# Attention scores of one head in one PSUM bank, issued in rounds of three matmuls, in a two-layer Mamba, attention and expert kernel

## The chip, the cores and the metric

The kernel runs on one core of one Trainium2 chip. The metric is the device time of one execution in microseconds. A core has five engines that run their own queues in order: TensorE (PE, matrix products into the accumulation memory PSUM), VectorE (DVE), ScalarE (ACT, table functions), GpSimd (POOL) and SyncE (SP, which issues DMAs). PSUM has eight banks; a bank holds 512 fp32 values for each of 128 partitions.

## The reference

A sequence of 2048 tokens of width 128 goes through four blocks, each with a layernorm ahead and a residual sum behind:

```python
x = x + mamba2(layernorm(x))        # 8 heads of 32, state 16: chunked state-space block with gate
nx = layernorm(x)                   # 16 heads of 8, causal attention
scores = einsum('bqhd,bkhd->bhqk', q, k) / sqrt(8)
x = x + softmax(where(causal, scores, min)) @ v @ Wo + bo
nx2 = layernorm(x)                  # 8 experts, the best two of each token, gates by softmax
for e in range(8):
    h = gelu(nx2 @ fc1_w[e].T + fc1_b[e])
    moe += (h @ fc2_w[e].T + fc2_b[e]) * dense_gates[..., e:e+1]
x = x + moe
x = x + mamba1(layernorm(x))        # h = dA * h + dB*u, state 16, summed over the state
x = x + mlp(layernorm(x))           # silu(w1 x) * (w2 x), two gelu layers, w3
```

## The kernel before

The 2048 tokens lie in four chunks of 512 (`C`). Each block handles a chunk at a time; causal attention of chunk `c` reads the keys of chunks 0 to `c`. Everything is traced in one program, so the order in which Python generators are advanced is the order of every engine's queue. The functions `ssd` (first block), `attentions`, `experts`, `scan` (third block) and `feed` (last block) are such generators; each `yield` carries a weight of planned work. `with_attention` advances the stages of other blocks and, for each weight it gets times `RATE`, steps of attention. So attention's instructions lie between those of the state-space block of later chunks, and later between those of experts, scans and feed-forward of earlier chunks. When attention ends, the tail runs: `scan(2)` with `experts(3)`, `scan(3)` with `feed(2)`, and `feed(3)` alone. Within attention, `in_step` advances two generators in turn:

- `weighted(c, g)` works on a group `g` of four heads. For each block of 128 keys it makes the transposed scores (line 352), adds each query's shift by a matmul with ones (line 358), adds the causal mask on the diagonal by a matmul (line 360), takes the exponential on ACT (line 362), and, one key block later, multiplies with the values (`sum_up`, line 339).
- `shift(c, g)` is one group ahead. It makes the scores a second time, with queries on the partitions (line 302), adds the mask (line 311), and takes the maximum over the keys on DVE (line 312); the negated maxima, split in two parts, are the shift that `weighted` adds.

A head has 8 features. With a split of each operand into high and low parts it fills 32 partitions, so the score matmuls of four heads lie on four row groups of PE, and those that are issued together run at once. Both generators work on pairs of heads: a tile of two banks takes the scores of heads `i` and `i + 1`, and one ACT or DVE instruction reads both (128 x 1024 values).

PSUM is shared out by tags (line 81): `m` has one buffer of two banks (the maximum's scores and attention's small products), `e` one of two banks (the weighted scores), `o` one bank (the sum over values), `a` two banks and `c` one bank (the other blocks). `whole` (line 141) gives a one-bank request the two-bank buffer of `m` or `e`. A `Stream` (line 657) names the tags that a stage of the second layer uses: `bank` goes round its `tags`, `sum` takes its `sums`. Stages beside attention use `a` and, for sums, `c`; in the tail `other` uses `m`, `e` and, for sums, `o`.

In `experts`, the gates of the chunk are transposed to rows (lines 757 to 774, with a high and a low part). For each expert a matmul `spread_row` copies one row to all 128 partitions (line 719), DVE copies it out (line 785), four products with GELU follow (lines 789, 790), then the second product (line 794) and its weighting by the gate (line 796). Weights come by SP's DMAs (lines 780, 781), and SP also fetches the broadcast rows `bb` of the scan (line 861) from a scratch in DRAM.

Of the kernel before, what the change touches and what calls it, by code (L numbers as in the profile page):

```python
# [12 lines left out]
F32 = mybir.dt.float32  # L13
# [59 lines left out]
def two_layers(ctx: ExitStack, tc: tile.TileContext, a: dict, out: bass.AP):  # L73
# [7 lines left out]
    BUFS = {"m": 1, "e": 1, "o": 1, "a": 2, "c": 1}  # L81
# [58 lines left out]

    def whole(tag, shape):
        if tag in ("m", "e") and len(shape) == 2 and shape[1] == C:
            return psum(tag, [shape[0], 2, C])[:, 0]
        return psum(tag, shape)
# [103 lines left out]

    def prepare(c):
# [13 lines left out]
        for g in range(0, NG, 2):  # L263
            qR.append(ak.tile([P, 2, C], F32R, tag="qR", name="qR", bufs=3))
            for w, n, dst in ((w_k, "k", kR[:, g : g + 2, cs]), (w_q, "q", qR[-1])):
                pf = psum("m" if n == "k" else "e", [P, 2, C])
                for j in range(2):
                    nc.tensor.matmul(pf[:, j], w[:, g + j], nT, start=True, stop=True)
                    hi = ak.tile([P, C], F32R, tag="os", name="hi")
                    nc.scalar.activation(hi, pf[:, j], AF.Identity, bias=col(f"b{n}", g + j))  # L270
                    nc.tensor.matmul(pf[:, j], minus[n], hi, start=False, stop=True, skip_group_check=True)
                    nc.vector.tensor_scalar(dst[:, j], pf[:, j], col(f"b{n}", g + j), None, ALU.add)
                yield 2.2
# [13 lines left out]
    def shift(c, g):  # L287
# [4 lines left out]
        for r in range(NB):  # L292
            w = (r + 1) * P
            top = sp.tile([P, 4, c + 1], F32, tag="top", name="top", bufs=4)
            for kc in range(c + 1):
                diag = kc == c
                n = w if diag else C
                for i in (2, 0):
                    pss = psum("m", [P, 2, C])
                    for j in range(2):  # L300
                        hr = slice(32 * (i + j), 32 * (i + j) + 32)
                        nc.tensor.matmul(  # L302
                            pss[:, j, 0:n],
                            qR[hr, w - P : w],
                            kR[hr, g, kc * C : kc * C + n],
                            start=True,
                            stop=not diag,
                        )
                    yield None
                    for j in range(2 * diag):  # L310
                        nc.tensor.matmul(pss[:, j, w - P : w], ident16, mask_qk, start=False, stop=True)
                    nc.vector.tensor_reduce(top[:, i : i + 2, kc], pss[:, :, 0:n], AX.X, ALU.max)  # L312
                    yield 0.4
# [13 lines left out]
    def weighted(c, g):  # L327
# [15 lines left out]

        for kb in range(nk):
# [3 lines left out]
            for i in range(0, 4, 2):  # L348
                pss = psum("e", [P, 2, C])
                for j in range(2):  # L350
                    hr = slice(32 * (i + j), 32 * (i + j) + 32)
                    nc.tensor.matmul(  # L352
                        pss[:, j, q0:], kR[hr, g, kb * P : (kb + 1) * P], qR[hr, q0:], start=True, stop=False
                    )
                yield None
                for j in range(2):
                    hr = slice(32 * (i + j), 32 * (i + j) + 32)
                    nc.tensor.matmul(pss[:, j, q0:], onesR[hr], sh[hr, q0:], start=False, stop=not diag)  # L358
                for j in range(2 * diag):
                    nc.tensor.matmul(pss[:, j, q0 : q0 + P], ident16, mask_kq, start=False, stop=True)  # L360
                pr = ak.tile([P, 2, C], F32, tag="probs", name="probs", bufs=3)
                last = nc.scalar.activation(  # L362
                    pr[:, :, q0:], pss[:, :, q0:], AF.Exp, scale=float(1.0 / np.sqrt(np.float32(HD)))
                )
                in_turn("exp", last)
                prs.append(pr)
                yield None

                if i == 0 and waiting:
                    sum_up(*waiting.pop())  # L370
                yield 1.1
            waiting.append((kb, q0, prs, last))
        sum_up(*waiting.pop())
# [81 lines left out]
    with ExitStack() as first:  # L455
# [36 lines left out]
        bigs, smalls = ["a", "a", "e"], ["c", "o", "m"]  # L492

        def big(shape):
            bigs.append(bigs.pop(0))
            return whole(bigs[-1], shape)

        def small_bank(shape):
            smalls.append(smalls.pop(0))
            return whole(smalls[-1], shape)  # L500
# [151 lines left out]
        bigs[:], smalls[:] = ["a"], ["c"]  # L652
# [4 lines left out]
    class Stream:  # L657
# [16 lines left out]
        def bank(self, shape):  # L674
            self.n += 1
            return whole(self.tags[self.n % len(self.tags)], shape)

        def sum(self, shape):
            return whole(self.sums, shape)
# [7 lines left out]
    side = Stream("", wk, 4, 6, ("a",), "c")  # L687
    scans = Stream("s", wk, 8, 4, ("a",), "c")
# [3 lines left out]
    w_bd = load(wp, "w_bd", [P, 2, 3 * DS], "(k p) o -> p k o", p=P)  # L692
    w_u = load(wp, "w_u", [P, 2, DI], "(k p) o -> p k o", p=P)
    w_dt1 = load(wp, "w_dt1", [3 * DS, DI])
# [7 lines left out]

    zeros = side.line("zeros")
    nc.gpsimd.memset(zeros, 0.0)
    two_rows, minus_low, rows_in = {}, {}, {}
    scratch_b = [tc.dram_tile([DS, C], F32, name=f"scratch_b{i}") for i in range(2)]
    for n in (NE,):
        two_rows[n] = wp.tile([P, n], F32R, name=f"two_rows{n}")
        nc.vector.tensor_tensor(two_rows[n], ident[:, 0:n], ident[:, n : 2 * n], ALU.add)
        minus_low[n] = wp.tile([2 * n, 2 * n], F32R, name=f"minus_low{n}")  # L710
# [368 lines left out]
```

## Time and profile before

| | |
|---|---|
| median of three runs | 1753.43 us (1750.17 to 1770.97) |
| profiled execution: its own time, span | 1741.55 us, 1739.8 us |
| mean granted clock of TensorE | 0.837 |
| busy: PE, DVE, ACT, POOL | 1466.9, 975.0, 726.2, 284.0 us |
| first and last exponential (line 362) | 162.7 and 1412.8 us |
| table loads ahead of line 362 | 41, of 1.28 us each |
| maximum (line 312), two full banks | 1222 ns, 224 of 320 |
| exponential (line 362), two full banks | 1024 ns, 224 of 320 |
| score matmuls, 512 columns (lines 302, 352) | 572 and 570 ns in the mean |
| shift matmuls, 512 columns (line 358) | 477 ns in the mean |
| copy of a gate row (line 785) | 24 of 679 ns, 8 in the tail |

The durations of matmuls are modelled from start to the end of their pipeline, and matmuls on different row groups overlap, so the busy time of PE is more than the time for which it takes in columns. The idle time of an engine stands with the instruction before which it stood idle, and behind an arrow what ended it.

### The profile page before, as it was taken

What the parts mean: (1) busy time and instruction counts of PE and PEld (TensorE: products, weight loads), DVE (VectorE), ACT (ScalarE), POOL (GpSimd) and SP (SyncE); (2) the same over time, 40 slices, a digit from 0 to 9 for tenths busy, and PEclk for the clock granted to TensorE, in tenths of its full rate; (3) what the DMA queues carried; (4) which work ended last, traced back from release to release, by engine and by line L of the source; (5) the groups of instructions that cost most, each with busy time, mean ns of one, the idle gap of its engine ahead of it and who ended that gap; (6) DMA issues with size and microseconds to landing.
All of it is one profiled execution on the core that took longest, in us unless ns stands there. A gap on an engine that the chain in (4) does not pass through costs nothing. (4 is left out here: it accounts for less than half of the span.)

```text
span 1739.8 us, 16427 instructions
## 1 busy us (share of the span) xinstructions
PE 1466.9 (84%) x6306; PEld 633.5 (36%) x6306; DVE 975.0 (56%) x1556; ACT 726.2 (42%) x847; POOL 284.0 (16%) x316
## 2 busy tenths in 40 slices
PE   6898999998999888888978887789999888658528
PEld 3554545444333333232333322433333233223214
DVE  4566646557344565667466686674442036774950
ACT  2222322322445444555354454355563536534522
POOL 3322210211000100112111021110000001440220
PEclk9898997887899978889677898669996899868859
DMA  2000000001000000324220045320011022860841
GB/s 85 1 1 1 1 1 1 1 1 55 24 25 25 25 13 21 83 49 103 55 49 14 30 99 107 68 42 25 24 37 31 24 67 78 178 125 31 188 96 30
DMA packets 62494, 83.24 MB, mean 48 GB/s; under 512 B 4576, under 2 KB 28816, under 8 KB 62416
## 3 DMA queue, kind: packets, MB, share of 16 engines
q0 software_dynamic: 16320, 31.46, 10.4%
q1 hardware_dynamic: 45664, 49.68, 9.7%
q8 instruction: 49, 0.80, 0.2%
q10 hardware_dynamic: 432, 1.06, 0.2%
q14 instruction: 29, 0.24, 0.0%
HBM read 49.55 MB, written 1.18 MB: 29 GB/s over the span
## 5 line engine op out<-in xcount | busy, mean ns | idle before, releaser
L362 ACT ACTIVATE probs<-ps_e 128x1024 f32<-128x1024 f32 (+3 forms) x320 | 286.6, 896 | 505.8 <-PE ps_e L358 304.0
L312 DVE TENSOR_REDUCE top<-ps_m 128x2 f32<-128x1024 f32 (+3 forms) x320 | 339.7, 1062 | 280.8 <-PE ps_m L302 164.1
L302 PE MATMUL ps_m<-kR,qR 32*128 32x512 f32 (+3 forms) x640 | 190.1, 523 | 68.0 <-DVE top L312 55.2
L352 PE MATMUL ps_e<-qR,kR 32*128 32x512 f32 (+3 forms) x640 | 175.5, 519 | 27.5 <-ACT probs L362 26.8
L339 PE MATMUL ps_o<-probs,vv 128*9 128x512 f32 (+3 forms) x1152 | 169.7, 599 | 1.0 <-ACT probs L362 0.9
L302 PEld LDWEIGHTS ps_m<-kR,qR 32*128 32x128 f32 x640 | 78.6, 208 | 242.9 <-DVE top L312 132.1
L867 DVE TENSOR_TENSOR_SCAN db<-da,hlast,db 128x512 f32<-128x512 f32 x128 | 163.0, 1310 | 6.5 <-ACT da L863 4.7
L358 PE MATMUL ps_e<-sh,onesR 32*128 32x512 f32 (+3 forms) x640 | 148.9, 431 | 0.0
L352 PEld LDWEIGHTS ps_e<-qR,kR 32*128 32x128 f32 x640 | 69.7, 204 | 182.0 <-ACT probs L362 106.3
L789 PE MATMUL ps_a<-nT,wide 128*128 128x512 f32 x192 | 113.8, 699 | 6.0 <-ACT h L790 3.7
L794 PE MATMUL ps_c<-h,wide 128*128 128x512 f32 x192 | 103.5, 643 | 0.0
L798 POOL TENSOR_TENSOR acc<-acc,ye 128x512 f32<-128x512 f32 x28 | 43.6, 1558 | 331.5 <-DVE ye L796 331.5
L871 POOL COPY hlast<-db 128x2 f32<-128x2 f32 x48 | 29.4, 612 | 378.9 <-DVE db L867 378.9
L863 ACT ACTIVATE da<-dl 128x1024 f32<-128x1024 f32 x64 | 66.4, 1054 | 51.5 <-DMA db<-db 28.3
L865 DVE TENSOR_TENSOR db<-du,bb 128x1024 f32<-128x1024 f32 x64 | 77.9, 1227 | 16.3 <-issue 11.0
L790 ACT ACTIVATE h<-ps_a,cols 128x512 f32<-128x512 f32 x96 | 63.8, 686 | 52.2 <-PE ps_a L789 51.9
L358 PEld LDWEIGHTS ps_e<-sh,onesR 32*128 32x128 f32 x640 | 77.2, 219 | 3.2 <-issue 1.8
L927 PE MATMUL ps_a<-g,wide 128*128 128x512 f32 x96 | 54.0, 690 | 19.5 <-ACT g L930 19.5
L789 PEld LDWEIGHTS ps_a<-nT,wide 128*128 128x128 f32 x192 | 37.1, 215 | 46.3 <-issue 19.5
L362 ACT ACT_TABLE_LOAD x41 | 52.6, 1283 | 1.3 <-PE ps_e L358 0.6
L927 PE MATMUL ps_a<-h,wide 128*128 128x512 f32 x96 | 51.1, 665 | 0.8 <-ACT g L930 0.8
L375 DVE COPY os<-ps_o 128x512 f32<-128x512 f32 x16 | 10.9, 684 | 70.8 <-PE ps_o L339 70.7
(375 smaller groups left out, 2129.3 us busy)
## 6 DMA issues: line engine op xcount, KB each, us to landing
wide<-in_fc SPq DMA_DIRECT2D x64, 256.0 KB, 3.2
bb<-scratch_b SPq DMA_DIRECT2D x64, 256.0 KB, 3.5
db<-db POOLq DMA_DIRECT2D x32, 512.0 KB, 5.7
u<-db POOLq DMA_DIRECT2D x28, 512.0 KB, 6.0
wide<-in_h SPq DMA_DIRECT2D x16, 512.0 KB, 3.7
wide<-in_w SPq DMA_DIRECT2D x8, 256.0 KB, 3.1
x<-in_x SPq DMA_DIRECT2D x4, 256.0 KB, 5.1
w<-in_w SPq DMA_DIRECT2D x4, 256.0 KB, 4.0
```

Of the source, the lines that this page charges most:

```text
L302: nc.tensor.matmul(pss[:, j, 0:n], qR[hr, w - P : w], kR[hr, g, kc * C : kc * C + n], start=True, stop=not diag,)
L312: nc.vector.tensor_reduce(top[:, i : i + 2, kc], pss[:, :, 0:n], AX.X, ALU.max)
L339: pv = nc.tensor.matmul(o, v, prs[i // 2][:, i % 2, q0:], start=kb == 0, stop=kb == nk - 1)
L352: nc.tensor.matmul(pss[:, j, q0:], kR[hr, g, kb * P : (kb + 1) * P], qR[hr, q0:], start=True, stop=False)
L358: nc.tensor.matmul(pss[:, j, q0:], onesR[hr], sh[hr, q0:], start=False, stop=not diag)
L362: last = nc.scalar.activation(pr[:, :, q0:], pss[:, :, q0:], AF.Exp, scale=float(1.0 / np.sqrt(np.float32(HD))))
L789: nc.tensor.matmul(ph, we[:, 0, f * P : (f + 1) * P], nT, start=True, stop=True)
L794: nc.tensor.matmul(py, we[:, 1, f * P : (f + 1) * P], hs[f // 2][:, f % 2, :], start=f == 0, stop=f == NF - 1)
L863: in_turn("exp", nc.scalar.activation(da, dl, AF.Exp, scale=-float(n + 1)))
L865: nc.vector.tensor_tensor(db, du, bb.unsqueeze(1).to_broadcast(two), ALU.mult)
L867: nc.vector.tensor_tensor_scan(db[:, j, :], da[:, j, :], db[:, j, :], hlast[:, j, n : n + 1], ALU.mult, ALU.add)
L927: nc.tensor.matmul(ph, w[k // 2][:, k % 2, f * P : (f + 1) * P], h[k // 2][:, k % 2, :], start=k == 0, stop=k == NF - 1)
```

## The change

Scores now stand in one bank for each head. `m` gets two buffers and `e` three, of one bank each; `c` is gone, and what used it takes `a`.

- In `shift`, each head has its own matmul, its own mask matmul and its own maximum (order 2, 3, 0, 1).
- In `weighted`, a step issues the shift of the head before (`shifted`), then the scores of this head; after the other generator's scores were issued, `finish` issues the mask and the exponential of the head before. `sum_up` follows in the second step of the next key block.
- `in_round` makes each of these matmuls depend on the second last reader noted for `m` and for `e`, so on the maximum and the exponential of two rounds ago.
- `prepare` makes its projections in one bank at a time.
- The rows of the gates go to a scratch in DRAM, and each expert's row comes back by a broadcasting DMA on SP, in place of the spreading matmul and the copy.
- The tail's `other` goes round five buffers of `m` and `e`; the first block's streams go round `a`, `e`, `o` and `m`; 16 unused rows of `bd` are dropped.

```diff
-    BUFS = {"m": 1, "e": 1, "o": 1, "a": 2, "c": 1}
+    BUFS = {"m": 2, "e": 3, "o": 1, "a": 2}
...
+    read = {"m": [], "e": []}
+
+    def in_round(matmul, depth={"m": 2, "e": 2}):
+        for tag, readers in read.items():
+            if len(readers) >= depth[tag]:
+                tc.add_manual_dep(matmul.ins, readers[-depth[tag]].ins.name, SYNC, reason="in one round")
...
-                for i in (2, 0):
-                    pss = psum("m", [P, 2, C])
-                    for j in range(2):
-                        hr = slice(32 * (i + j), 32 * (i + j) + 32)
+                for i in (2, 3, 0, 1):
+                    hr = slice(32 * i, 32 * i + 32)
+                    pss = psum("m", [P, C])
+                    in_round(
                         nc.tensor.matmul(
-                            pss[:, j, 0:n],
...
+                            pss[:, 0:n], qR[hr, w - P : w], kR[hr, g, kc * C : kc * C + n], start=True, stop=not diag
                         )
+                    )
                     yield None
-                    for j in range(2 * diag):
-                        nc.tensor.matmul(pss[:, j, w - P : w], ident16, mask_qk, start=False, stop=True)
-                    nc.vector.tensor_reduce(top[:, i : i + 2, kc], pss[:, :, 0:n], AX.X, ALU.max)
-                    yield 0.4
+                    if diag:
+                        nc.tensor.matmul(pss[:, w - P : w], ident16, mask_qk, start=False, stop=True)
+                    read["m"].append(nc.vector.tensor_reduce(top[:, i, kc : kc + 1], pss[:, 0:n], AX.X, ALU.max))
+                    yield 0.2
...
+        def finish(kb, diag, q0, i, pss, pr):
+            if diag:
+                nc.tensor.matmul(pss[:, q0 : q0 + P], ident16, mask_kq, start=False, stop=True)
+            last = nc.scalar.activation(
+                pr[:, i % 2, q0:], pss[:, q0:], AF.Exp, scale=float(1.0 / np.sqrt(np.float32(HD)))
+            )
+            read["e"].append(in_turn("exp", last))
+            return last
+
+        def shifted(kb, diag, q0, i, pss, pr):
+            hr = slice(32 * i, 32 * i + 32)
+            in_round(nc.tensor.matmul(pss[:, q0:], onesR[hr], sh[hr, q0:], start=False, stop=not diag))
...
+            for i in range(4):
+                hr = slice(32 * i, 32 * i + 32)
+                if i % 2 == 0:
+                    prs.append(ak.tile([P, 2, C], F32, tag="probs", name="probs", bufs=3))
+
+                if begun:
+                    shifted(*begun)
+                pss = psum("e", [P, C])
+                in_round(
+                    nc.tensor.matmul(pss[:, q0:], kR[hr, g, kb * P : (kb + 1) * P], qR[hr, q0:], start=True, stop=False)
+                )
                 yield None
...
+                if begun:
+                    last = finish(*begun)
+                begun = (kb, diag, q0, i, pss, prs[-1])
+
+                if i == 0 and kb:
+                    waiting.append((kb - 1, q_before, prs_before, last))
+                if i == 1 and waiting:
                     sum_up(*waiting.pop())
-                yield 1.1
...
+                yield 0.55
...
-        gT = rows_in[NE][0]
...
+        gT = z.line("gT", (NE, C))
+        nc.vector.tensor_copy(gT, pgt)
+        gates = scratch_g[c % 2]
+        nc.sync.dma_start(gates, gT)
         yield 1.5
...
             we = z.wide()
             nc.sync.dma_start(we[:, 0], a["fc1"][e])
             nc.sync.dma_start(we[:, 1].rearrange("p (k d) -> p k d", k=NF), a["fc2"][e].rearrange("(k p) d -> p k d", p=P))
-            pg = z.bank([P, C])
-            spread_row(pg, NE, gT, e)
             gb = z.line("gb")
-            nc.vector.tensor_copy(gb, pg)
+            nc.sync.dma_start(gb, gates[e].partition_broadcast(P))
...
-        other = Stream("o", pool, 6, 8, ("m", "e"), "o")
+        other = Stream("o", pool, 6, 8, ("m", "e", "m", "e", "e"), "o")
```

## The prediction

> **What bounds the kernel now.** I read the page first, then the windows by stage, then the waits of TensorE (PE), then single rounds in the timeline, and last the costs of single forms.
>
> ```profile
> span 1739.8 us, 16427 instructions
> ...
> PE 1466.9 (84%) x6306; PEld 633.5 (36%) x6306; DVE 975.0 (56%) x1556; ACT 726.2 (42%) x847; POOL 284.0 (16%) x316
> ```
>
> ```profile
> 160.00:1415.00 1255.00, 1123.35 (x5224) 460.72 (x5222) 690.33 (x1073) 556.61 (x642) 154.65 (x172) 0.83 0.15 36
> 1415.00:1740.00 325.00, 211.47 (x540) 95.71 (x538) 193.27 (x243) 135.67 (x147) 79.96 (x68) 0.81 0.47 106
> ```
>
> The columns of the windows are the stretch, its length, then busy time and count of PE, PEld, DVE, ACT and POOL, the granted clock, the DMA share and GB/s. In the attention stage (160 to 1415) PE is busy for 90% of the time and no other engine for over 55%. In the tail (1415 on) it is 65%, and the chain of waits is made of scans, their exponentials and accumulating DMAs. So PE counts before 1415, and a chain through DVE, ACT and DMA after it.
>
> A busy PE is not an efficient one. The timeline shows why, for two neighbouring rounds:
>
> ```profile
> 904.71 0.49 PE L302 MATMUL ps_m<-kR,qR 32*128 32x512 f32 x2
> ...
> 906.77 0.50 PE L302 MATMUL ps_m<-kR,qR 32*128 32x512 f32 x2 [1.09 <-DVE top L312]
> ...
> 907.11 0.39 PE L352 MATMUL ps_e<-qR,kR 32*128 32x512 f32 x2
> ...
> 907.34 0.40 PE L358 MATMUL ps_e<-sh,onesR 32*128 32x512 f32 x2
> ...
> 907.77 1.22 DVE L312 TENSOR_REDUCE top<-ps_m 128x2 f32<-128x1024 f32 x1
> 907.84 1.02 ACT L362 ACTIVATE probs<-ps_e 128x1024 f32<-128x1024 f32 x1 [1.03 <-PE ps_e L358]
> ```
>
> Two things are to be seen. One round takes 906.77 - 904.71 = 2.06 us, because the single m buffer makes PE wait until the 1.22 us maximum has read it. And the six matmuls of 32 rows, which sit on four row groups, came as three batches 0.34 and 0.23 us apart, because m and e came free at different moments. I took the matmuls of lines 302, 352 and 358 of the attention stage in order of start, and called those that start within 30 ns of each other a batch: 903 batches. The ideal is two for each of the 320 rounds, 640; all four score matmuls started together in only 61 rounds.
>
> PE's time in that stage then splits so. Back-to-back fp32 matmuls of 512 columns (L927) start 0.43 us apart at full clock; I take that as their stream, half of it (0.215) for a 32-row batch, and divide by the granted clock. Streams come to 855 us (445 attention, 410 the other work), waits of over 0.35 us to 171, of which 117 stand before attention's score matmuls, and short gaps to 228.
>
> ```profile
> PE ps_m L302 <- DVE top L312: 55.2, 55, 3.6
> ...
> PE ps_e L352 <- ACT probs L362: 26.8, 25, 3.4
> ...
> PE ps_e L789 <- DVE gb L785: 10.5, 3, 4.8
> ...
> PE ps_m L789 <- DVE gb L785: 8.9, 2, 6.3
> ```
>
> These waits (total, times, longest) are PE's own idle time, so they leave out latency inside a matmul. The last two lie in the tail.
>
> **The change, part by part.** The sum is made against the profiled execution's own 1741.55 us; the median of three runs, 1753.43, lies 11.9 above it and I add 12 at the end.
>
> *Batches.* After the change a round is one head: the shift of head i-1, the scores of head i, the maximum's scores of head i+2. These are three row groups and three banks, issued with nothing between them, and the first waits for both the maximum and the exponential of two rounds ago, so the others find their events done. That is about 640 batches, plus some 64 where maxima run alone as a block gets longer: 704 in place of 903. One batch less saves 0.215/0.84 = 0.26 of stream and 0.105 of gap (mean of the short gaps ahead of a separate L358 batch): 199 x 0.36 = **-72 us**. Bounds: -95 (640) and, if rounds split, a loss (third rival).
>
> *Masks.* The count of mask matmuls stays (512), but they now follow single heads. Gaps between a row batch and a mask were 199, of 0.16 us in the mean. With 256 masks on each side, and about 133 rounds in which both sides are on the diagonal, there are 512 - 133 = 379: 180 x 0.16 = **+29 us**. Bounds: 0, since these gaps may be absorbed where PE waits anyway, and +58 at twice the gap.
> The Trainium skill, in "TensorEngine Tiling (Array Packing)", section "Key Properties", says that a change of tiling mode drains TensorE, and speaks against this part. Read strictly, each new switch would drain on the way in and on the way out; the trace shows gaps on the way in and almost none on the way out. By the rule the term would be 58 and my total 29 higher.
>
> *Waits.* m and e have two and three buffers, so PE may run one round ahead while DVE and ACT read. Single banks cost them more, as these forms show:
>
> ```profile
> L312 DVE TENSOR_REDUCE top<-ps_m 128x2 f32<-128x1024 f32 x224 | 273.7, 1222 | 198.8 <-PE ps_m L302 164.1 <-PE ps_m L311 25.0 <-PE ps_e L358 9.3
> L362 ACT ACTIVATE probs<-ps_e 128x1024 f32<-128x1024 f32 x224 | 229.3, 1024 | 372.4 <-PE ps_e L358 304.0 <-PE ps_e L360 61.4 <-PE ps_m L302 6.5
> ...
> L312 DVE TENSOR_REDUCE top<-ps_m 128x2 f32<-128x512 f32 x32 | 22.0, 688 | 23.9 <-PE ps_m L311 23.9
> ...
> L362 ACT ACTIVATE probs<-ps_e 128x512 f32<-128x512 f32 x32 | 19.1, 597 | 34.6 <-PE ps_e L360 34.3
> ```
>
> Where attention runs alone, two heads then need 2 x 0.688 of DVE plus some 0.1 of gaps, about 1.5 us in place of 2.06. The rest of the 117 us comes from a reader that is late behind other work in its own queue (a scan pair of 2.5 us, a table load of 1.28), which one round of slack doesn't cover. I take half: **-58 us**. Bounds: 0 and -117. What is queued behind the waiting first matmul is all of PE: sums over V and the experts' matmuls too, as now. The sum over V now waits for an exponential issued one round before it, which I count in the half that stays.
>
> *ACT and DVE work.* 320 x (2 x 0.597 - 1.024) = 54 us more ACT and 320 x (2 x 0.688 - 1.222) = 49 more DVE, less 32 gate copies of 0.68 = 22. The cover is PE's 90%: DVE is at 55% and ACT at 44% in the stage. But DVE reaches 73% from 1000 to 1100, so I charge **+10**. Bounds: 0 and +54 (no cover).
> The same page's section "PSUM Bottleneck" says that PSUM reads may become the limit once tiling is used and that they should be vectorised over tiles, which is the opposite of this edit. The idle times above agree only in part, since both readers mostly waited for PE; by the rule all 103 us would be on the path.
>
> *Gates by DMA.* 32 spreading matmuls and 32 copies go; 32 loads of 256 KB and 4 small writes come, all on SP. In attention 24 matmuls of 0.26 + 0.13 give **-9 us**. The loads land in 3.5 us (as bb from its scratch) and are needed only after eight or more fp32 matmul streams of 0.43 us; should that cover fail, 24 x 0.5 = 12 is lost. The write, however, waits for gT, and the first expert's weights queue behind it on SP; now they were fetched some 20 us ahead (1419 for a use at 1440). Issue and landing, about 4.5 us, less the attention steps scheduled there: 3 x 2 = **+6**, bounds 0 and +14. The transposes in place of the hi/lo pair: 0 (a copy and a matmul fewer, hidden by attention steps).
>
> *Bank c gone.* Sums now take turns in a. An expert's sum is read by a 0.75 us DVE instruction, and about 4 us of attention is placed between it and the second matmul that wants the bank; before, the gate copy held a bank in just the same way. The opening has one more bank to rotate over. **0**, bounds -10 and +15.
>
> *Tail.* PE no longer waits for the gate copies (10.5 + 8.9) and the experts get five banks in place of two; their late GELUs hold up the scan's exponentials on ACT. Some -15, and +5 for the weights' late fetch, with no attention to cover it: **-10**, bounds -30 and +10 (the gate loads share the engines with the accumulating DMAs).
>
> *Clock.* Streams were paid at 0.84 of full clock. Fewer waits may raise it, fewer batches may lower it: **0**, and 0.04 either way (twice the difference of the two stages) gives 855 x (1 - 0.84/0.88) = -39 at 0.88 and +43 at 0.80.
>
> Sum: -72 + 29 - 58 + 10 - 9 + 6 - 10 = -104. 1741.55 - 104 = 1637.6, and with 12 for the runs, 1650.
>
> **The rivals.**
> *First, the waits stay (1705 to 1740; taken 1725).* Batches merge, but a reader that is late because of scans and table loads is late for the new round as well, and ACT and DVE pay their extra 54 + 49 - 22 = 81 us partly where PE waits; I charge 30, over half of the 54. Then -72 + 29 + 0 + 30 - 9 + 6 - 10 = -26, or 1727 on the scale of the runs. For it: the longest waits reach 3.6 us, more than two short rounds. Against it: most are near 1 us (55.2/55).
> *Second, a larger gain (1526).* The full -95, -100 of waits, a clock near 0.88 and -20 in the tail give 1741.55 - 95 + 29 - 100 - 9 + 6 - 39 - 20 + 12 = 1526. For it: a half-clock stretch began in the middle of such waits (908 us). Against it: 410 us of other streams on PE don't change.
> *Third, the other side: rounds split.* If the three matmuls of a round don't start together, for instance because a mask or a third event lies between them, PE pays 0.36 us for each extra batch. My other terms of the attention stage and the tail come to -32. From 903 + 32/0.36, about 990 batches, the gain is gone: that is so if over some 290 of the 704 rounds split in two. If all 640 full rounds split, there are 1344, or +159: 1741.55 + 159 - 32 + 12 = 1880; if two thirds do, 1805. For it: 842 of the present batches hold fewer than four. Against it: 1184.68 shows matmuls of m and e starting in the same 10 ns once both events had come.
> *Fourth: the change doesn't do what it says.* Rounds in which one stream has no partner (the last group, the longer blocks) are few, 64 of 704; that is inside the bounds.
>
> **How the numbers follow.** The forecast 0.43 and the second rival 0.12, both faster by over 2%; the first 0.20; the third 0.25. Two per cent is about what a measurement of this kernel can tell from no change. Faster by over 2% (below 1718): 0.55; within 2%: 0.20; slower (above 1788): 0.25. The likeliest case's own range is 1580 to 1700. The range that should hold 8 in 10 goes from 1565 to 1800.
>
> **What would show it.** Right: score and shift matmuls in threes with one start, near 704 batches; waits of L302's and L352's successors on the maximum and the exponential cut in half; the maximum at 0.69 and the exponential at 0.60 us, 640 of each; attention over near 1320 in place of 1415; no wait for gb. Wrong: more than 990 batches, PE waits on ACT and DVE that grew with their busy time, mask gaps twice as many and as long, or weight loads that PE waits for at each expert block's start.

## The result and the profile after

The change made the kernel slower: 1806.99 us median (1806.3 to 1817.16) against 1753.93 for the kernel before beside it, a ratio of 1.0297 with a 95% interval of 1.022 to 1.0373. The forecast was 1650. A run over 1.5% above the fastest of its kernel counts as slow and is left out of the ratios, so a ratio need not be the quotient of the medians given with it. The page of the profiled execution (1806.3 us) and its two windows by stage:

```profile
span 1804.6 us, 17226 instructions
PE 1547.9 (86%) x6254; PEld 667.8 (37%) x6254; DVE 985.3 (55%) x1832; ACT 765.8 (42%) x1167; POOL 275.0 (15%) x315
```

```profile
160.00:1415.00 1255.00, 1151.95 (x4960) 473.36 (x4959) 707.26 (x1366) 559.74 (x900) 148.96 (x172) 0.79 0.16 40
1415.00:1804.00 389.00, 263.45 (x805) 115.07 (x803) 190.96 (x235) 174.81 (x214) 77.70 (x68) 0.84 0.43 98
```

ACT and DVE grew by 40 and 10 us and have nearly as much room as before. PE grew by 81, with 52 matmuls fewer in the record, and in the attention stage its granted clock fell from 0.83 to 0.79. The last exponential ends at 1481.2 us in place of 1413.2, and what follows it takes 323.3 in place of 326.6: the loss lies in the attention stage. The two profiled executions lie 65 us apart, the medians 53: the one of before is 12 us faster than its median, and what is read from the two profiles holds these 12 us too.

The new rounds do what was said, where nothing lies between them. The timeline of PE after, in the region without a diagonal, shows shift, scores and the maximum's scores with one start, here at half clock:

```profile
987.49 0.79 PE L356 MATMUL ps_e<-sh,onesR 32*128 32x512 f32 x1
987.50 0.79 PE L372 MATMUL ps_e<-qR,kR 32*128 32x512 f32 x1
987.50 0.79 PE L306 MATMUL ps_m<-kR,qR 32*128 32x512 f32 x1
```

On the diagonal it is otherwise. Here is the timeline of PE before, and then that after:

```profile
1185.02 0.40 PE L358 MATMUL ps_e<-sh,onesR 32*128 32x512 f32 x2
1185.35 0.29 PE L360 MATMUL ps_e<-mask_kq,ident 128*128 128x128 bf16 x2
```

```profile
255.15 0.44 PE L372 MATMUL ps_e<-qR,kR 32*128 32x384 f32 x1
255.15 0.38 PE L306 MATMUL ps_m<-kR,qR 32*128 32x256 f32 x1
255.52 0.23 PE L347 MATMUL ps_e<-mask_kq,ident 128*128 128x128 bf16 x1
255.59 0.22 PE L312 MATMUL ps_m<-mask_qk,ident 128*128 128x128 bf16 x1
```

Before, two masks followed two heads. Now every round of one head ends in masks on the whole array, so PE goes from row groups (32 rows) to a mask (128 rows) 342 times in place of 199, and straight back from a mask to row groups 212 times in place of 18.

The costliest shapes of the two readers, the masks (after the bar: busy us, mean ns) and PE's waits:

```profile
L313 DVE TENSOR_REDUCE top<-ps_m 128x1 f32<-128x512 f32 x448 | 297.2, 686 | 184.9 <-PE ps_m L306 133.8 <-PE ps_m L312 30.7 <-PE ps_e L356 13.1
L348 ACT ACTIVATE probs<-ps_e 128x512 f32<-128x512 f32 x448 | 256.3, 596 | 403.0 <-PE ps_e L356 160.9 <-PE ps_m L306 111.1 <-PE ps_e L347 92.0
...
L312 PE MATMUL ps_m<-mask_qk,ident 128*128 128x128 bf16 x256 | 63.1, 247 | 0.0
L347 PE MATMUL ps_e<-mask_kq,ident 128*128 128x128 bf16 x256 | 61.4, 240 | 0.0
```

```profile
PE ps_e L356 <- DVE top L313: 44.6, 59, 5.6
PE ps_o L780 <- ACT h L776: 36.1, 6, 11.7
...
PE ps_o L340 <- ACT probs L348: 13.9, 26, 1.3
...
PE ps_e L356 <- ACT probs L348: 3.4, 7, 0.8
```

The readers take what was said (686 and 596 ns) and mostly wait for PE. Before its scores and shifts PE waits less for the exponential than it did (3.4 in place of 26.8), but the sum over values (L340) now waits 13.9 for it, where it was 0.9. The wait for the maximum, now ahead of L356, is nearly as large as before (55.2). The waits for the gate copies (10.5 and 8.9 in the tail) are gone with the copies; in their place the experts' second product (L780) waits 36.1 us for GELU in the tail, where before it waited 0.9 and the first products (L789) some 7.5.

**PE's time in the attention stage.** I split it as the prediction did: a batch is a set of score, shift or maximum's matmuls with one start, a stream the time for columns (at full clock, then at the granted one), a wait an excess of over 0.35 us, a gap a smaller one. "Of it masks" are the gaps from row groups to a mask and back. Streams are estimates, since they use the prediction's 0.43 and 0.215 us for 512 columns. From 160 us on, streams at the granted clock, gaps and waits add up to the stage's end within 2 us.

| kernel | stage's end | streams full, at clock | gaps (of it masks) | waits | batches | us at half clock |
|---|---|---|---|---|---|---|
| before | 1413.2 | 707.5, 853.5 | 227.3 (35) | 171.6 | 903 | 423 |
| after | 1481.2 | 701.6, 890.8 | 273.0 (102) | 157.4 | 824 | 527 |
| after, no wait for the round | 1455.0 | 753.4, 910.3 | 293.8 (112) | 89.0 | 1092 | 415 |
| after, neither wait nor masks | 1395.4 | 727.5, 879.7 | 210.8 (0) | 145.4 | 1081 | 385 |
| before, gates by DMA | 1420.8 | 705.7, 850.0 | 229.9 (35) | 180.8 | 903 | 420 |
| the same, maxima by one head | 1491.7 | 741.7, 954.0 | 271.1 (73) | 106.8 | 1122 | 547 |
| before, zero matmuls | 1399.8 | 759.6, 856.2 | 238.4 (35) | 145.3 | 850 | 263 |
| after, zero matmuls | 1452.7 | 751.5, 875.7 | 295.9 (95) | 120.5 | 811 | 344 |

After less before, the 68 us are, within 1: streams at full clock -6, the lower clock +43 (890.8 - 701.6 = 189 lost to it, where it was 853.5 - 707.5 = 146), mask gaps +68, other gaps -22, waits -14.

### The profile page after: what moved, and what is told of

Read it like the earlier page. It is cut to its first block, busy times and chain, and to the rows that moved or that the text cites. A ratio compares the mean times of both kernels' runs of the same rounds, so it can differ in the third digit from the quotient of the medians.

```text
span 1804.6 us, 17226 instructions
## 1 busy us (share of the span) xinstructions
PE 1547.9 (86%) x6254; PEld 667.8 (37%) x6254; DVE 985.3 (55%) x1832; ACT 765.8 (42%) x1167; POOL 275.0 (15%) x315
## 4 chain that ended last, share of the span: by engine, by line
PE 63%; DVE 17%; issue 7%; ACT 6%; DMA 4%; POOL 2%; SPq 0%; POOLq 0%; DVEq 0%; ACTq 0%
PE ps_e L356 9%; PE ps_o L340 9%; PE ps_a L775 6%; DVE db L853 5%; PE ps_a L780 4%; DVE top L313 4%; PE ps_m L306 3%; DMA db<-db 3%; PE ps_a L913 3%; ACT probs L348 2%; PE ps_e L347 2%; DVE db L851 2%; PE ps_a L563 2%; PE ps_a L580 1%; PE ps_a L605 1%
## 5 line engine op out<-in xcount | busy, mean ns | idle before, releaser
L348 ACT ACTIVATE probs<-ps_e 128x512 f32<-128x512 f32 (+3 forms) x640 | 329.4, 532 | 566.5 <-PE ps_e L347 232.0
L313 DVE TENSOR_REDUCE top<-ps_m 128x1 f32<-128x512 f32 (+3 forms) x640 | 376.3, 606 | 281.4 <-PE ps_m L306 133.8
L356 PE MATMUL ps_e<-sh,onesR 32*128 32x512 f32 (+3 forms) x640 | 319.4, 522 | 58.5 <-DVE top L313 44.6
L306 PE MATMUL ps_m<-kR,qR 32*128 32x512 f32 (+3 forms) x640 | 319.1, 526 | 3.9 <-DVE att L398 2.0
L372 PE MATMUL ps_e<-qR,kR 32*128 32x512 f32 (+3 forms) x640 | 302.8, 542 | 2.4 <-DVE xa L409 1.4
L356 PEld LDWEIGHTS ps_e<-sh,onesR 32*128 32x128 f32 x640 | 130.7, 213 | 318.5 <-ACT probs L348 106.0
L340 PE MATMUL ps_o<-probs,vv 128*9 128x512 f32 (+3 forms) x1152 | 179.7, 630 | 15.1 <-ACT probs L348 13.6
L306 PEld LDWEIGHTS ps_m<-kR,qR 32*128 32x128 f32 x640 | 131.6, 216 | 44.1 <-issue 18.8
L372 PEld LDWEIGHTS ps_e<-qR,kR 32*128 32x128 f32 x640 | 120.8, 210 | 19.0 <-issue 11.4
L780 PE MATMUL ps_a<-h,wide 128*128 128x512 f32 x192 | 97.1, 631 | 0.4 <-ACT sz L870 0.4
L780 PE MATMUL ps_o<-h,wide 128*128 128x512 f32 x64 | 37.3, 732 | 36.2 <-ACT h L776 36.1
L312 PE MATMUL ps_m<-mask_qk,ident 128*128 128x128 bf16 x256 | 63.1, 247 | 0.0
L347 PE MATMUL ps_e<-mask_kq,ident 128*128 128x128 bf16 x256 | 61.4, 240 | 0.0
```

The source lines that it names most:

```text
L306: nc.tensor.matmul(pss[:, 0:n], qR[hr, w - P : w], kR[hr, g, kc * C : kc * C + n], start=True, stop=not diag)
L313: read["m"].append(nc.vector.tensor_reduce(top[:, i, kc : kc + 1], pss[:, 0:n], AX.X, ALU.max))
L340: pv = nc.tensor.matmul(o, v, prs[i // 2][:, i % 2, q0:], start=kb == 0, stop=kb == nk - 1)
L347: nc.tensor.matmul(pss[:, q0 : q0 + P], ident16, mask_kq, start=False, stop=True)
L348: last = nc.scalar.activation(pr[:, i % 2, q0:], pss[:, q0:], AF.Exp, scale=float(1.0 / np.sqrt(np.float32(HD))))
L356: in_round(nc.tensor.matmul(pss[:, q0:], onesR[hr], sh[hr, q0:], start=False, stop=not diag))
```

## The experiments

Ratios are to the kernel before, run on the same chip, with their 95% intervals.

**The masks, left out of both kernels.** The edit in the kernel after (in the kernel before, the same with the pair's loops):

```diff
-                    if diag:
-                        nc.tensor.matmul(pss[:, w - P : w], ident16, mask_qk, start=False, stop=True)
...
-            if diag:
-                nc.tensor.matmul(pss[:, q0 : q0 + P], ident16, mask_kq, start=False, stop=True)
```

> The kernel before, with the causal mask matmuls (lines 311 and 360) left out, so that diagonal blocks are not masked. It sets the base for the next run. Masks theory: a mask costs its stream (31 us in the stage, at the granted clock) and the gaps around it (32 us ahead, 13 behind), so about 75 us, some 1680. Rounds theory (the loss comes from the rounds of three themselves): the same here.

> The kernel after, with the mask matmuls left out in the same way. Masks theory: nearly all of the 53 us between the two kernels are switches between row groups and the whole array (gaps ahead of a mask 342 of 0.22 us in place of 199 of 0.16, gaps behind them 34 us in place of 13) and the lower clock that follows; then this run lies within 15 us of the kernel before without masks, at about 1680. Rounds theory: it stays 40 us or more above it, at 1720 or more.

Measured: 1747.9 us, 0.9857 [0.9751, 0.9963], and 1754.83 us, 0.9984 [0.9938, 1.0031]. The level of about 1680 that the masks theory gave fell: without its masks the kernel before gains 1.4%, not 75 us. The kernel after gains 3.1%, so the difference between the two shrinks from 2.97% to 1.27%, and some 30 of 53 us go. The 22 us that stay are over the 15 of the masks theory and under the 40 of the rounds theory. That share is rough: the four runs of the kernel before without masks go from 1723 to 1751 us, and its ratio rests on two of them. The change still doesn't gain: the masks are not the whole cause.

**The wait for the round, taken away** (each matmul then waits for its own bank alone):

```diff
-            if len(readers) >= depth[tag]:
+            if len(readers) >= 10**9:
```

> The kernel after without the added dependencies of in_round; each matmul waits only for what its bank and operands need. If the common events are what makes matmuls start in threes and this is worth something: slower than after by 10 us or more, at 1820 or more, with more batches than 824. If the coupling costs more than it brings (the shift waits for a maximum that it does not need): faster by 10 us or more, 1795 or less. If neither: 1807 within 8.

> The kernel after without in_round and without the mask matmuls (diagonal blocks are not masked). The trace of after without in_round shows 81 us of gaps ahead of masks and 31 behind them, waits of 89 us in place of 157, and 1092 batches. Two causes that add up (switches to masks; waits that the common events bring): some 75 us below that run's 1789, at 1715, with waits still near 90 us. If the masks were what in_round suffered from, so that without masks the rounds pay: slower than the kernel after without masks (1755) or equal to it.

Measured: 1789.35 us, 1.016 [1.01, 1.0219], and without masks 1723.12 us, 0.9837 [0.9782, 0.9893]. With masks and without them, the kernel is some 1.4 to 1.5% faster when rounds don't wait. Without this wait the masks cost 3.2%, and with both gone the kernel (0.9837) is no slower than the kernel before without masks (0.9857). The 1715 forecast for it was close; its waits, 145 us, were not near the 90 expected. PE's waits for the two readers in the first of the two:

```profile
PE ps_e L372 <- ACT probs L348: 21.0, 42, 2.3
PE ps_m L306 <- DVE top L313: 14.7, 25, 4.0
```

The table shows the trade. Waiting for both readers saves 268 batches (1092 to 824) and 52 us of streams at full clock, and costs 68 us of waits (89 to 157) and 112 us more at half clock.

**The gates by DMA alone**, in the kernel before:

```diff
-            pg = z.bank([P, C])
-            spread_row(pg, NE, gT, e)
             gb = z.line("gb")
-            nc.vector.tensor_copy(gb, pg)
+            nc.sync.dma_start(gb, gates[e].partition_broadcast(P))
```

> The kernel before with only the gates' rows moved to the scratch in DRAM and the broadcasting DMA. By the prediction's terms: 9 us less in attention, 6 more for late weights, about 10 less in the tail: 1741 on the scale of the runs. If this part is where the loss comes from (weights that queue on SP behind the write of the gates): 1780 or more.

Measured: 1736.27 us, 0.9838 [0.9763, 0.9913]. This part helps. Where is not to be seen in the profiles: the profiled executions of this kernel and of before have nearly the same span (1739.4 and 1739.8 us), and PE's waits in the tail for the gate copies give way to 27.0 us of waits for GELU. The profile's DMA issues of this kernel (KB each, median us to landing):

```profile
gb<-scratch_g SPq DMA_DIRECT2D x32, 256.0 KB, 4.1
```

**Bank c given up**, with and without the gates by DMA, everything else as before:

```diff
-        bigs, smalls = ["a", "a", "e"], ["c", "o", "m"]
+        bigs, smalls = ["a", "a", "e"], ["a", "o", "m"]
...
-        bigs[:], smalls[:] = ["a"], ["c"]
+        bigs[:], smalls[:] = ["a"], ["a"]
...
-    side = Stream("", wk, 4, 6, ("a",), "c")
-    scans = Stream("s", wk, 8, 4, ("a",), "c")
+    side = Stream("", wk, 4, 6, ("a",), "a")
+    scans = Stream("s", wk, 8, 4, ("a",), "a")
```

> The kernel before with the gates by DMA and with bank c left unused: sums and small products of the other blocks take a, as after. What is left between this run and after is the scores' own change. Prediction's term for c: 0, so 1736 within 10. If the missing bank is a part of the loss: 1755 or more.

> The kernel before with only bank c left unused (sums and small products of the other blocks take a). From the pair of runs with the gates by DMA, c is worth 1.012 - 0.984 = 2.8%: some 1800. If the bank mattered only because of the gates' DMA: within 15 us of before.

Measured: with the gates by DMA 1773.1 us, 1.012 [1.004, 1.02], so 2.8% above the same kernel with its bank; without, 1782.93 us, 1.0157 [1.0124, 1.019]. The second is a cost too, but neither of the two forecast ones (some 1800, or within 15 us of before). I had costed this part at nothing. Then each of the three users gave up the bank alone (the edit's first two hunks, its `side` line, its `scans` line), beside gates by DMA:

> The kernel before with the gates by DMA; only the state-space block gives up bank c for its sums and takes a. Theory one (the state-space block pays, because its chains of small products and sums alternate most closely, and its chunks end 23 to 57 us later after the change): 1.005 to 1.012 of before, half-clock time unchanged, PE's waits in the attention stage near 200 us in place of 181. Rival (the payer is another): 0.982 to 0.988, so 1723 to 1734 us.

> The kernel before with the gates by DMA; only the experts and the feed-forward give up bank c and take a for their sums. Theory one (the state-space block pays): 0.982 to 0.988 of before. Rival two (an expert's accumulation now stands in a bank that two products of the next expert want): over 1.0, with new waits of PE on the products of GELU.

> The kernel before with the gates by DMA; only the scans give up bank c and take a for their output product. Theory one: 0.982 to 0.988 of before, since a chunk has one such product. Rival three (the meeting of scans and experts on two banks is the price): over 1.0, with the lag arising between 900 and 1000 us, where a scan and experts run abreast.

Measured: 0.9927 [0.9892, 0.9962] for the state-space block, 0.9983 [0.9951, 1.0015] for the experts and the feed-forward, 0.9925 [0.9879, 0.9971] for the scans. Each of the three theories forecast over 1.0 for its own payer and 0.982 to 0.988 for the others, and none came true. Against the 0.9838 of the kernel with its bank the three lie 0.9, 1.5 and 0.9% higher, which adds up to 3.2%, near the 2.8% of all three together. So the price is spread over the users, and no single one pays it. The two of 0.9% are hardly clear of noise by themselves, since their intervals still touch that of 0.9838.

In the profiles the attention stage ends 12 us later when all three give up the bank beside gates by DMA, and 32 us later without them; the tail is 6 us longer in both. What holds PE up in the attention stage was not found. In the tail one wait is new where the experts' and the feed-forward's sums use a:

```profile
PE ps_a L909 <- ACT sz L856: 15.1, 2, 13.7
```

The feed-forward's last product (L909) takes a bank of a that holds a scan's product until ACT reads it (L856). That wait of 13 to 14 us stands in the tail of every profiled kernel in which these sums use a, that after included (L923, 13.5), and in none where they keep c. That it lengthens the tail is not shown: in this kernel the longest wait of the scan's own product falls from 26.9 to 8.3 at the same time, and its tail of 323.5 us lies within the 318.6 to 324.8 us of five kernels with gates by DMA that keep bank c.

**The maxima alone by one head**, beside gates by DMA; the weighted side keeps pairs and bank c, and `in_step` advances the maxima twice as often for each of its steps:

```diff
-    BUFS = {"m": 1, "e": 1, "o": 1, "a": 2, "c": 1}
+    BUFS = {"m": 2, "e": 1, "o": 1, "a": 2, "c": 1}
...
-                for i in (2, 0):
-                    pss = psum("m", [P, 2, C])
...
+                for i in (2, 3, 0, 1):
+                    pss = psum("m", [P, C])
...
-                    nc.vector.tensor_reduce(top[:, i : i + 2, kc], pss[:, :, 0:n], AX.X, ALU.max)
-                    yield 0.4
+                    nc.vector.tensor_reduce(top[:, i, kc : kc + 1], pss[:, 0:n], AX.X, ALU.max)
+                    yield 0.2
```

> The kernel before with gates by DMA and c kept, and only the maximum's side of the change: two m buffers of one bank, one head for each matmul, mask and DVE maximum, without added dependencies; the weighted side stays in pairs. If waits for the single m buffer are what bounds (57 us of PE's own idle time): 20 us or more below 1736. If more switches to masks and more batches take it back: 1736 or more.

Measured: 1815.28 us, 1.0266 [1.0169, 1.0362], 4.3% above gates by DMA. PE's waits for the two readers, which were 57.3 and 28.1 with gates by DMA alone:

```profile
PE ps_m L302 <- DVE top L308: 27.4, 49, 3.1
PE ps_e L348 <- ACT probs L358: 17.2, 23, 1.9
```

The waits of the stage fell from 181 to 107 us, and the stage is 71 us longer: 219 more batches put 36 us of streams at full clock and 41 of gaps in, and the clock took 68 more. Here a buffer that removed waits of PE wasn't worth it, since it split batches.

**Weighted masks by GpSimd**, after the exponential, in place of mask matmuls (on the kernel with gates by DMA, and on the change without its wait for the round):

```diff
-                    nc.tensor.matmul(pss[:, j, q0 : q0 + P], ident16, mask_kq, start=False, stop=True)
+                    select(pr[:, :, q0 : q0 + P], [[0, 2], [1, P]], 0, -1, ALU.is_ge, 0.0)
```

> The kernel before with the gates by DMA, and the mask of the weighted scores taken off TensorE: GpSimd sets the future keys' probabilities to zero after the exponential. Switch theory: half of the masks' stream (13 us) and gaps (20 us) and some clock, 30 to 40 us less than with the gates alone, about 1700. If GpSimd, which waits in its queue for the experts' and the scans' results, is late with it: 1736 or more, with waits of the sums over V for GpSimd.

> The kernel after without in_round and with the weighted scores' mask on GpSimd after the exponential, as in the run beside it. Switch theory: half of 81 + 31 us of gaps less what stands there without a mask, and 13 us of stream: 40 to 60 us below 1789, at 1730 to 1750. GpSimd late: 1789 or more.

Measured: 1735.93 us, 0.9899 [0.9831, 0.9967], no different from 0.9838; and 1755.83 us, 1.0014 [0.9974, 1.0054], 1.5% below the kernel that it started from. Half of the masks taken off PE are worth 1.5% where heads are single and nothing where they are pairs. So the switch theory missed in the first (30 to 40 us forecast) and came short in the second (34 us in place of 40 to 60). GpSimd's results are sometimes late, but PE's sums wait just 4.0 and 2.8 us for them, and their weight loads 11.7 and 19.4. In the first, PE's streams and gaps fell by 23 us at full clock, and the time at half clock rose from 420 to 457.

**Matmuls that nobody needs.** PE's clock in these traces is either full or half. If a thinly filled PE loses its clock, more columns should bring time back. In the first kernel (gates by DMA, no bank c) 320 matmuls write the free bank and aren't read; in the others 256 or 512 matmuls with zero weights add nothing to the sum over values:

```diff
+                nc.tensor.matmul(psum("c", [P, C]), ident16, fill16, start=True, stop=True)
...
+                for _ in range(1 if kb > 1 else 0):
+                    nc.tensor.matmul(po, zero16, fill16, start=False, stop=False, skip_group_check=True)
```

> The kernel before with gates by DMA and c unused by the others (the run that lay at 1773), plus one bf16 matmul of 512 columns on the whole array ahead of each pair of weighted scores, into the free bank c, whose result nobody reads: 320 more streams of 0.213 us at full clock, 68 us, and as many switches. Theory that the granted clock follows the share of time in which PE streams: half-clock time in the attention stage falls from 416 us to 350 or less, and the time grows by less than 50 us. Theory that the clock does not depend on it: half-clock time stays within 30 us of 416, and the time grows by 80 us or more, less what lands in waits.

> The kernel after with one matmul of zeros (bf16, 512 columns, whole array) added onto the sums' bank in every second step from the third key block on, 272 in all, 58 us of streams at full clock; the sums don't change. Clock theory: after loses 43 us by its lower clock (527 us at half clock in the stage, 423 before); with the streams half-clock time falls below 420 us, and the time comes down by 30 us or more from 1807. If after's loss lies in gaps and waits alone: 1807 or more, as the streams add to it.

> The kernel before with the same matmuls of zeros, one ahead of each pair of weighted scores from the third key block on. Clock theory: half-clock time from 423 to some 300 us, and 20 to 40 us less than before, some 1720. Otherwise: 1755 or more. With the run beside it: if the clock carries a part of the difference between the two kernels, it shrinks from 53 us to 35 or less.

> The kernel before with the gates by DMA, c kept, and the matmuls of zeros. If the two gains add up: 0.984 x 0.977, about 1690, faster than both kernels. If the streams only fill what the gates' part had gained: 1727.

> As the run beside it with two matmuls of zeros in a row, 544 in all, 116 us of streams at full clock. If the clock still gains by them: within 10 us of the run beside it or faster. If the waits and the clock are used up: 30 us or more slower than that run.

| kernel | us | ratio |
|---|---|---|
| gates by DMA, no bank c, and filler | 1734.37 | 0.988 [0.9842, 0.9918] (1.012 without) |
| before, zero matmuls | 1731.17 | 0.9866 [0.9821, 0.9911] |
| after, zero matmuls | 1780.82 | 1.0161 [1.0122, 1.02] |
| gates by DMA, zero matmuls | 1722.88 | 0.9831 [0.9791, 0.9871] |
| gates by DMA, two zero matmuls each | 1739.26 | 0.9918 [0.9889, 0.9947] |

The zero matmuls' group in the kernel before with them, and the core's span and clock without them and with them:

```profile
L354 PE MATMUL ps_o<-fill,zero 128*128 128x512 bf16 x256 | 102.9, 407 | 0.0
```

```profile
core 0: 1739.8 us, clock 0.837
```

```profile
core 0: 1730.7 us, clock 0.875
```

Added work makes three kernels faster, by 1.3 to 2.4%: the streams of the kernel before grow by 52 us at full clock and by 3 at the granted one. Not all of the gain is clock: its batches and waits fell too (903 to 850, 171.6 to 145.3 us). In the kernel after the time at half clock fell as forecast (527 to 344 us), the time itself by 26 us, a little less than the 30 forecast. The fourth, gates by DMA, stays where it was (0.9838 and 0.9831), and a second zero matmul makes it 16 us slower, between the two forecasts; so gains don't add up. And the hope that this would also close the distance between the kernels fell: 1780.82 less 1731.17 is 50 us, against 53 without zero matmuls. That the clock is what separates the two kernels is thus not shown; in the table's stage it takes 28 us of their 53 with zero matmuls, the mask gaps 60, and the waits give 25 back. The kernel with gates by DMA, with zero matmuls or without, beats both: some 1.6% below before.

## Why the prediction was wrong

**The steps that failed.** The sum promised -100 us for the attention stage (-72 - 58 + 29 + 10 - 9), and the profiles show +68. By the split above, four terms make this: batches (-28 for -72, 44 us off), waits (-14 for -58, 44 off), the clock (+43 for 0) and the switches to the masks (+68 for +29, 39 off). Bank c, put at 0, costs 28 to 49 us by the runs; its price stands inside these terms and isn't to be added to them.

**What bounds it: right.** PE sets the attention stage, a chain the tail; ACT and DVE kept their cover: their extra work, 40 and 10 us where I had 54 and 27, is small beside their idle time, and their readers mostly wait for PE. One wait for ACT grew: the sum over values waits 13.9 us for exponentials in place of 0.9, and 3.3 when rounds don't wait. So no 103 us of PSUM reads came onto the path, as would follow from the prediction's reading of the section "PSUM Bottleneck" of the Trainium skill's "TensorEngine Tiling (Array Packing)"; that section's advice is for tiles in the same bank, and the two heads of a pair stood in two.

**Batches (-72): the count failed, not the price.** I expected 704 batches and there are 824: 377 hold just one of each kind, but 115 are a maximum's scores alone, 67 a shift alone. That streams fell by 6 and gaps other than the masks' by 22 is -28 us, which is 79 batches at my 0.36. Masks don't make the splits: without masks there are 817. What does was not settled. (Of the 903 batches before, 815 hold fewer than four matmuls; the prediction's 842 are those that aren't the four score matmuls.)

**Masks (+29): more than twice the term.** My count held (379 foreseen, 342 gaps), but they took 0.224 us each in place of 0.164, and I called the way out "almost none". Before, only 18 masks were followed by a row batch at once, and the gaps there were 0.11 us: they were few, not short. With single heads 212 gaps of 0.12 stand there. The term measures 44 + 24 = +68. Here the trace agrees with the Trainium skill, in "TensorEngine Tiling (Array Packing)", section "Key Properties": a change of tiling mode drains TensorE. I had set aside my strict reading of it, by which each switch costs on the way in and on the way out, and had worked out +58 from it.

**Waits (-58): my half was a guess, and it was -14.** A round that waits for both readers is as late as the later of them. The rows to go by were there: a table load of 1.28 us on ACT or a pair of scan steps of 2.5 us on DVE, ahead of either reader, can hold up three matmuls now. The runs without this wait show the choice plainly: the waits go (89), the batches come back (1092), and the net is a gain of 1.4%.

**Gates by DMA: better than the sum.** My terms for them (-9, +6 and most of the tail's -10) come to some -13; alone they give -1.6%, some -28 us; where was not found. The loads land in about 4 us and are hidden, as said, and no wait for gb is left among PE's largest.

**Bank c gone (0, bounds -10 and +15): outside its bounds.** It costs 28 to 49 us (1.6 to 2.8%). I looked at an expert's sum alone and didn't follow the other users' sums one by one; by the runs each of the three users pays a part. What PE waits for instead is shown only for the feed-forward's product in the tail (13.5 us), and not that this wait counts; the rest stays open.

**Tail (-10): -3.3, too little to tell from nothing.** Kernels that differ little in the tail have profiled tails 6 us apart. PE's waits for the gate copies (19.4 us) are gone, but 36.1 us of waits for GELU and the 13.5 just named came in; I had reckoned with the first alone.

**Clock (0, +43 at 0.80): at its bound.** The stage was granted 0.79, which makes the +43 of the split above. A part of it may be the choice of the run: runs of before alone were granted between 0.819 and 0.838 in one series of 25, and the profiled one 0.837. Between 400 and 500 us the clocks of before and after differ most, though after is late there and does other work than before:

```profile
400.00:500.00 100.00, 93.06 (x420) 41.11 (x419) 49.81 (x106) 40.97 (x51) 9.37 (x14) 0.88 0.14 40
```

```profile
400.00:500.00 100.00, 96.67 (x427) 47.25 (x426) 54.66 (x136) 26.31 (x53) 12.28 (x20) 0.71 0.09 24
```

PE is "busy" for longer, at a lower clock. 58 of the 68 us have arisen by the end of the state-space block's last chunk, at 477 in place of 420 us. But the kernel with gates by DMA, which does nearly the same work as before up to there, ends it at 435: two executions of nearly the same instructions can differ by some 15 of these 58 us.

**In per cent of the kernel before**, going from one part to the next: gates by DMA -1.6, bank c +2.8, and all the rest, single banks in rounds, +1.8, of which the wait for the round is 1.4. That makes the 3.0. The switches to the masks are in that rest; so are projections in one bank and the other rotation of buffers in the opening and the tail, which were not run alone. The parts need not add up in another order, since masks and the wait were measured inside the whole change.

**The rivals.** The first had the waits right and nothing else. The third was on the right side by another way: its price needed 990 batches, and there were 824. By the runs three things that I priced at 0, +29 and -58 make the change slow: a bank (1.6 to 2.8%), the switches to the masks (some 1.7%) and the common wait (1.4%). The lower clock goes with them; as a cause of its own it was not isolated.

## What to carry to other kernels

A PSUM bank that is taken from other users has a price in all of them: list each user's next product and what holds its bank then, the tail's too, before it is set to nothing. When matmuls on row groups are cut into finer rounds, count the switches to full-array matmuls in both directions, and don't tie several matmuls to the latest of several readers unless the batches saved outweigh the waits kept. Take a part out of a large change and run it alone: here one part gained 1.6% under a loss of 3.0%.

## What the runs showed of the hardware

*A PE that waits for nothing long still loses its clock.* The granted clock in these traces is 1 or one half, and its intervals are multiples of 3.41 us. I took for each such window of before and after the share of time in which PE takes in columns. Windows after which the clock fell had a share of 0.31 in the median, nine in ten below 0.45; windows that kept full clock had at least 0.53 in nine of ten; a half clock returned to full only after shares near 0.8 and above. That is what the traces show together, not a cause shown by itself; the runs with zero matmuls fit it (423 us at half clock fall to 263).

The Trainium skill, in "TensorE: Matmul & The Clock Gate", section "HAM oscillation — how this bites in real kernels", has the clock fall when TensorE is idle for over about 3.4 us. The window's length and the two clocks agree with these traces; that only such a silence does it they don't bear out. In the attention stage of before just three stretches without a running matmul reach 3.4 us (the longest 3.6), PE's waits for the maximum are near 1 us in the mean (55.2 us in 55), and yet the clock falls 34 times and is at one half for 423 us.

*Reading one bank by itself costs more than half of reading two.* The maximum takes 686 ns for one full bank and 1222 for two, the exponential 596 and 1024; but both engines mostly waited for PE, so little of this price is seen in the time.
